# First attention of a two-layer network in half steps, with two strips of each score pass side by side

## The chip, the cores and the metric

The kernel runs on one core of one Trainium2 chip. The metric is the device time of one execution in microseconds (us), lower is better; a shown time is the median of the runs of one kernel. The core has a matrix engine (PE, with its weight loads listed apart as PEld), a vector engine (DVE), a scalar engine (ACT), GpSimd (POOL) and a queue engine for transfers (SP). Each engine works through its own list of instructions in the order of the program; semaphores hold an instruction until what it needs is there. Products of PE land in PSUM, which the kernel uses as eight banks of 128 x 512 float32 numbers; DVE and ACT read them from there.

## What is computed

Eight sequences of 512 positions with 256 channels go through two layers, each an attention and a feed-forward part with modulated layer norms and gates. The change touches the first attention alone: 16 query heads of 16 channels, one key and one value head shared by all of them, rotary positions, a causal mask.

```python
h = _layernorm(x, axis=-1) * (1 + ca) + sa
q = (h @ Wq + bq).reshape(B, T, 16, 16); k = (h @ Wk + bk)[:, :, None, :]; v = (h @ Wv + bv)[:, :, None, :]
q, k = _apply_rope(q, sin, cos, 16), _apply_rope(k, sin, cos, 16)
att = jnp.einsum('bthd,bThd->bhtT', q, k) / math.sqrt(16)
att = jax.nn.softmax(jnp.where(causal, -jnp.inf, att), axis=-1)
out = jnp.einsum('bhtT,bThd->bthd', att, v).reshape(B, T, 256)
x = x + ga * (out @ Wo + bo)
```

After it come a layer of 16 experts that each choose 64 positions of every sequence, a linear attention with running sums, and three rounds of a coupling network.

## The kernel before, in words

**Two passes over the scores.** For each sequence, called a batch here, the score products are made twice. The first pass (`maxima`, lines 637 to 691) makes the scores with queries on the partitions and takes each row's maximum. The second pass (`heads_of`, lines 693 to 760) makes them again with keys on the partitions, subtracts the maxima by small bf16 products, takes the exponential, and multiplies with the values. The heads lie in four groups of 32 partitions: strip j (0 to 3) holds the scores made from partitions 32j to 32j+31. A product with 32 rows uses one of four row sets of PE, so products of different strips can run beside each other. A strip is one PSUM bank of 512 columns.

**Rounds.** The causal blocks of 512, 384, 128 and 256 columns are packed into five rounds of one or two blocks that fill 512 columns; there are two halves g of the heads, so ten rounds in each pass. A round of the first pass: four strips get their score products (line 644), then four or eight bf16 products with all 128 rows, an identity times a triangular mask of -1e30 (line 652), hide the upper triangle of the diagonal blocks, and four DVE reductions (lines 659, 666) read the strips. A round of the second pass: four strips of score products (line 723), the small products that subtract the maxima (line 731), four exponentials on ACT into `e` (line 738), one or two selections on POOL that zero the masked corner (line 742). Four value products with 128 rows by 32 columns (line 708, `values`) collect a batch's output; three of them stand between rounds, the fourth at the end.

**Steps.** The order on every engine is written out by hand: a batch is a Python generator, `Steps.run` takes one piece of each live generator per step, in order of rank, and the instructions stand in that order on each engine. A new batch starts every 15 steps (`steps.start_every(15, batch, 1)`). Batch b goes through `made_ready` (layer norm, transposes at line 263, QKV products at 564, rotation on DVE and POOL, transposes at 604 and 614), `maxima`, `heads_of`, and `finished` (transposes at 774 and 789, normalisation on DVE at 779 and 781, output product at 803, second layer norm, router product at 829). So in one step there stand a piece of `finished` of batch b-1 or so, a piece of `made_ready`, one round of the second pass of batch b, and one round of the first pass of batch b+1. The experts start when the second pass of the last batch is done (`until("heads", B - 1)`).

**Banks.** All PSUM tiles of this part come from one pool of eight banks (`net.mm()`). A new tile takes the bank that was released first, and its first product waits for the instruction that read the former tile last. A step takes four strips for each pass and one or more tiles for the other pieces, so nine or ten in all. Work for the end of the maxima (lines 673 to 689) turns them into three bf16 parts, transposes these (686) and copies them (`mT`, 689), which the second pass of that batch needs.

Of the kernel before, what the change touches and what calls it, by code (L numbers as in the profile page):

```python
# [11 lines left out]
F32 = mybir.dt.float32  # L12
# [8 lines left out]
P = 128  # L21
# [345 lines left out]
class Steps:  # L367


    def __init__(self):  # L370
        self.starters, self.lanes, self.past = [], [], set()
        self.count = 0

    def start(self, lane, rank):

        self.lanes.append([rank, self.count, lane])
        self.count += 1

    def start_every(self, every, batch, rank):
        def starter():  # L380
            for b in range(B):
                self.start(batch(b), rank)
                for _ in range(every):
                    yield

        self.starters.append(starter())

    def rank(self, rank):

        self.now[0] = rank  # L390
# [5 lines left out]
    def run(self):  # L396
        while self.starters or self.lanes:
            self.starters = [s for s in self.starters if next(s, self) is not self]
            for at in sorted(self.lanes, key=lambda at: at[:2]):
                self.now = at  # L400
                if next(at[2], self) is self:
                    self.lanes.remove(at)

# [11 lines left out]
def layer0(net, steps):  # L415
# [48 lines left out]
    for j in range(4):  # L464
# [8 lines left out]
    mask = wp.tile([P, P], F32, name="mask_qk")  # L473
    nc.gpsimd.memset(mask, 0.0)
    nc.gpsimd.affine_select(
        out=mask, in_=mask, compare_op=ALU.is_ge, fill=NEG,
        base=0, pattern=[[-1, P]], channel_multiplier=1,
    )
    maskb = wp.tile([P, P], BF16, name="maskb")
    nc.vector.tensor_copy(maskb, mask)  # L480
# [148 lines left out]

    def maxima(b, kT, qT):  # L630
# [6 lines left out]
        for g in range(2):  # L637
            for blocks in rounds:
                strips = [net.mm() for _ in range(4)]
                for n, (p, a, at) in enumerate(blocks):  # L640
                    i = tile_of[a]
                    nk = (i + 1) * P
                    for j in range(4):
                        nc.tensor.matmul(  # L644
                            strips[j][:, at : at + nk],
                            qT[rows_of(j), g, i * P : (i + 1) * P], kT[rows_of(j), p, :nk],
                            start=(n == 0), stop=False, skip_group_check=True,
                        )
                for j in range(4):
                    for p, a, at in blocks:  # L650
                        last = at + tile_of[a] * P
                        nc.tensor.matmul(  # L652
                            strips[j][:, last : last + P], net.identb, maskb,
                            start=False, stop=True, skip_group_check=True,
                        )
                p, a, _ = blocks[0]
                for j in range(4):
# [35 lines left out]
    def heads_of(b, kT, qT, mT):  # L693
# [7 lines left out]
        def values(n):  # L701

            av = net.mm()
            for a in range(4):
                c = chunk_of[a]
                e, at = parts.pop((n, a))
                for j in range(4):
# [4 lines left out]
                    )  # L712
            o = op.tile([P, T], F32, name=f"oT{n}")
            nc.scalar.copy(o, av)
            oT.append(o)

        for g in range(2):
            for r, blocks in enumerate(rounds):
                strips = [net.mm() for _ in range(4)]
                for n, (p, a, at) in enumerate(blocks):  # L720
                    c = chunk_of[a]
                    for j in range(4):
                        nc.tensor.matmul(  # L723
                            strips[j][:, at : at + T - c * P],
                            kT[rows_of(j), p, c * P : (c + 1) * P], qT[rows_of(j), g, c * P :],
# [1113 lines left out]
```

## Time and profile before

| | |
|---|---|
| median of 3 runs | 1199.55 us (1198.77 to 1199.65) |
| profiled execution | 1200.28 us, of which the span of the core is 1198.3 us |
| mean granted TensorE clock | 0.965 |
| busy: PE, DVE, ACT, POOL | 1105.7, 710.3, 554.7, 496.8 us |
| first product of the first pass, batches 0 to 7 | 28.4, 72.7, 124.7, 183.3, 241.8, 300.3, 358.8, 417.4 us |
| first product of the second pass, batches 0 to 7 | 70.4, 122.8, 181.4, 239.9, 298.4, 356.9, 415.6, 469.1 us |
| last value product of batch 7 | 504 us |
| experts, then second layer's attention and coupling | about 504 to 730, then to 1198 us |

The first attention thus takes the first 504 us or so of the span. A *period*, from the first product of the first pass of one batch to that of the next, is 58.5 us for batches 2 to 6. A busy time in a table of groups counts overlapping records of one group once; a matmul's record lasts longer than the time after which the next one may start, so the sum over groups is a little more than the time they take. The weight loads (PEld) run beside the products.

### The profile page before, as it was taken

What the parts mean: (1) busy time and instruction counts of PE and PEld (TensorE: products, weight loads), DVE (VectorE), ACT (ScalarE), POOL (GpSimd) and SP (SyncE); (2) the same over time, 40 slices, a digit from 0 to 9 for tenths busy, and PEclk for the clock granted to TensorE, in tenths of its full rate; (3) what the DMA queues carried; (4) which work ended last, traced back from release to release, by engine and by line L of the source; (5) the groups of instructions that cost most, each with busy time, mean ns of one, the idle gap of its engine ahead of it and who ended that gap; (6) DMA issues with size and microseconds to landing.
All of it is one profiled execution on the core that took longest, in us unless ns stands there. A gap on an engine that the chain in (4) does not pass through costs nothing. (4 is left out here: it accounts for less than half of the span.)

```text
span 1198.3 us, 22165 instructions
## 1 busy us (share of the span) xinstructions
PE 1105.7 (92%) x8942; PEld 712.4 (59%) x8942; DVE 710.3 (59%) x1463; ACT 554.7 (46%) x1024; POOL 496.8 (41%) x539
## 2 busy tenths in 40 slices
PE   4879999999999999879898999799999988999996
PEld 3545666665666665468776876466666665444433
DVE  4967676666666766723562223666667655556765
ACT  2145656565555547614332244444444324555444
POOL 3023334434343425466787787355556444000000
PEclk8889999999999999989999999899999998999998
DMA  6200000100001010198757944400000000000202
GB/s 215 65 9 2 2 28 25 28 24 28 27 26 42 12 48 23 52 295 234 180 83 187 245 79 60 107 7 6 5 6 5 6 2 1 0 1 1 71 0 71
DMA packets 67974, 69.09 MB, mean 58 GB/s; under 512 B 10216, under 2 KB 64544, under 8 KB 67872
## 3 DMA queue, kind: packets, MB, share of 16 engines
q1 hardware_dynamic: 55024, 49.32, 13.2%
q0 software_dynamic: 12288, 16.79, 8.2%
q8 instruction: 70, 1.15, 0.4%
q10 hardware_dynamic: 560, 1.58, 0.4%
q14 instruction: 32, 0.26, 0.1%
HBM read 46.38 MB, written 21.01 MB: 56 GB/s over the span
## 5 line engine op out<-in xcount | busy, mean ns | idle before, releaser
L738 ACT ACTIVATE e<-mm 128x512 f32<-128x512 f32 x320 | 164.7, 605 | 103.2 <-PE mm L731 99.3
L666 DVE TENSOR_REDUCE pm<-mm 128x4 f32<-128x512 f32 x256 | 158.8, 683 | 84.9 <-PE mm L652 84.6
L742 POOL TENSOR_SCALAR_AFFINE_SELECT e<-e 128x512 f32<-128x512 f32 x128 | 80.3, 645 | 252.3 <-ACT e L738 252.3
L644 PE MATMUL mm<-kT,qT 32*128 32x128 f32 (+3 forms) x1024 | 136.5, 467 | 1.5 <-DVE o_tok L781 1.4
L1112 POOL DMA_INDIRECT xs<-y,slot x64 | 101.4, 1585 | 38.9 <-issue 14.6
L723 PE MATMUL mm<-qT,kT 32*128 32x128 f32 (+3 forms) x1024 | 106.5, 465 | 0.0
L644 PEld LDWEIGHTS mm<-kT,qT 32*128 32x128 f32 x1024 | 75.2, 187 | 44.8 <-DVE pm L666 10.9
L1625 PE MATMUL mm<-g,cn_w 128*128 128x512 f32 x192 | 98.5, 627 | 0.0
L708 PE MATMUL mm<-e,vaug 128*32 128x512 f32 (+3 forms) x1024 | 77.3, 436 | 3.9 <-POOL e L742 2.5
L723 PEld LDWEIGHTS mm<-qT,kT 32*128 32x128 f32 x1024 | 57.1, 184 | 26.8 <-issue 10.6
L1044 POOL DMA_INDIRECT tok<-xg,gidx x64 | 63.4, 991 | 19.3 <-issue 17.5
L1668 DVE SCALAR_TENSOR_TENSOR m<-th,slope,g 128x512 f32<-128x512 f32 x48 | 34.0, 748 | 60.5 <-ACT th L1661 60.5
L1445 POOL TENSOR_SCALAR_AFFINE_SELECT am<-am 128x1024 f32<-128x1024 f32 x32 | 44.3, 1386 | 56.0 <-ACT am L1443 56.0
L1089 PE MATMUL mm<-ew,hid 128*128 128x256 f32 x256 | 63.9, 394 | 3.5 <-ACT hid L1078 3.5
L1076 DVE TENSOR_SCALAR hid<-mm,eb 128x512 f32<-128x512 f32 x32 | 24.0, 751 | 70.8 <-PE mm L1069 41.0
L1078 ACT ACTIVATE hid<-mm,eb 128x512 f32<-128x512 f32 x32 | 22.0, 686 | 92.5 <-PE mm L1069 77.2
L1069 PE MATMUL mm<-tokT,ew 128*128 128x256 f32 x256 | 62.0, 386 | 0.0
L1069 PE MATMUL mm<-hid,ew 128*128 128x256 f32 x256 | 61.4, 383 | 0.0
L1273 PE MATMUL mm<-hT,w1qkv 128*128 128x512 f32 x128 | 60.5, 618 | 0.0
L1094 DVE SCALAR_TENSOR_TENSOR y<-mm,eb,gb 128x512 f32<-128x512 f32 x32 | 23.9, 746 | 59.7 <-PE mm L1089 49.8
L1625 PEld LDWEIGHTS mm<-g,cn_w 128*128 128x128 f32 x192 | 33.6, 195 | 41.3 <-issue 39.5
L1089 PEld LDWEIGHTS mm<-ew,hid 128*128 128x128 f32 x256 | 48.4, 199 | 10.3 <-ACT hid L1078 4.3
(245 smaller groups left out, 2195.3 us busy)
## 6 DMA issues: line engine op xcount, KB each, us to landing
ew<-in_L_ffn_w SPq DMA_DIRECT2D x72, 256.0 KB
x<-in_L_attn_x SPq DMA_DIRECT2D x8, 512.0 KB
xs<-x SPq DMA_DIRECT2D x8, 512.0 KB
xg<-xh SPq DMA_DIRECT2D x8, 512.0 KB
x<-xs SPq DMA_DIRECT2D x8, 512.0 KB
out<-res SPq DMA_DIRECT2D x16, 256.0 KB
ga_row<-gate_a SPq DMA_DIRECT2D x16, 128.0 KB
mod_row<-rows SPq DMA_DIRECT2D x16, 128.0 KB
```

Source lines behind the costliest of these rows:

```text
L644: nc.tensor.matmul(strips[j][:, at : at + nk], qT[rows_of(j), g, i * P : (i + 1) * P], kT[rows_of(j), p, :nk], start=(n == 0), stop=False, ...
L666: nc.vector.tensor_reduce(pm[:, j, 2 * g + p, first : first + 4], strips[j].rearrange("q (a k) -> q a k", k=P), AX.X, ALU.max,)
L708: nc.tensor.matmul(av[32 * j : 32 * j + 32, c * P :], va[:, c, :], e[:, j, at : at + T - c * P], start=(a == 0), stop=(a == 3), skip_group ...
L723: nc.tensor.matmul(strips[j][:, at : at + T - c * P], kT[rows_of(j), p, c * P : (c + 1) * P], qT[rows_of(j), g, c * P :], start=(n == 0), ...
L738: nc.scalar.activation(e[:, j, :], strips[j], AF.Exp, scale=scale)
L742: nc.gpsimd.affine_select(out=own, in_=own, compare_op=ALU.is_ge, fill=0.0, base=0, pattern=[[0, 4], [1, P]], channel_multiplier=-1,)
L1044: nc.gpsimd.indirect_dma_start(out=tok[i][:, n, :], out_offset=None, in_=net.xg[half], in_offset=bass.IndirectOffsetOnAxis(ap=self.gidx[ha ...
L1069: nc.tensor.matmul(ps[:, o * C : (o + 1) * C], w[i][n][:, k, o * P : (o + 1) * P], src[:, k, :], start=(k == 0), stop=(k == 1),)
L1089: nc.tensor.matmul(ps[:, n * C : (n + 1) * C], hid2[i][:, k, n * P : (n + 1) * P], w[i][2][:, k, :], start=(k == 0), stop=(k == 1),)
L1112: nc.gpsimd.indirect_dma_start(out=net.xs[2 * half + n], in_=y[i][:, n, :], in_offset=None, out_offset=bass.IndirectOffsetOnAxis(ap=self.s ...
L1273: nc.tensor.matmul(ps, w[:, k, n * P : (n + 1) * P], hT[:, k, :], start=(k == 0), stop=(k == 1))
L1625: nc.tensor.matmul(ps, w1[:, k, o * P : (o + 1) * P], g[k][bb], start=(k == 0), stop=(k == 1),)
```

## The change

What it does, in words:

- `Steps.run` now counts half steps. A generator has a period (`every`) and a phase: most take a turn in every second half step, `made_ready` in the odd ones, `finished` in the even ones, the two score passes in all. A batch starts every 30 half steps, the second layer's attention every 34.
- A score pass may hand over groups of products instead of issuing them. `run` collects those of the two passes and issues them in turns: a group of the second pass, a group of the first, and so on. Then the readers are issued.
- A round is done in two half steps of two strips: strips 0 and 1 of the first pass beside 2 and 3 of the second, then the other way round. Both passes follow one ORDER of ten rounds with three pauses; in a pause the second pass makes a value product (in two halves), the first pass does nothing.
- The mask is four products of 32 rows for each strip, on the strip's own row set, in place of one or two of 128 rows. Their operands (`picks`, `hides`, 128 x 320 in bf16) are shifted views. Two diagonal blocks of a strip are one product of 256 columns. There are 160 mask products in a batch, with 64 before.

```diff
@@ Steps
-    def start_every(self, every, batch, rank):
+    def start_every(self, every, batch, rank, phase=0):
...
     def run(self):
+        step = 0
         while self.starters or self.lanes:
             self.starters = [s for s in self.starters if next(s, self) is not self]
+            together = []
             for at in sorted(self.lanes, key=lambda at: at[:2]):
+                if step % at[3] != at[4] % at[3]:
+                    continue
+                self.now = at
+                got = next(at[2], self)
+                if got is self:
+                    self.lanes.remove(at)
+                elif got is not None:
+                    together.append((at, got))
+            for groups in itertools.zip_longest(*(got for _, got in together), fillvalue=()):
+                for issue in itertools.chain(*groups):
+                    issue()
+            for at, _ in together:
                 self.now = at
                 if next(at[2], self) is self:
                     self.lanes.remove(at)
+            step += 1
@@ layer0
-    mask = wp.tile([P, P], F32, name="mask_qk")
...
-    maskb = wp.tile([P, P], BF16, name="maskb")
-    nc.vector.tensor_copy(maskb, mask)
+    wide = P + 2 * 96
+    picks = wp.tile([P, wide], BF16, name="picks")
+    hides = wp.tile([P, wide], BF16, name="hides")
+    for t, fill, keep in ((picks, 1.0, ALU.not_equal), (hides, NEG, ALU.is_ge)):
+        f = wp.tile([P, wide], F32, name="picks_f")
+        nc.gpsimd.memset(f, 0.0)
+        nc.gpsimd.affine_select(
+            out=f, in_=f, compare_op=keep, fill=fill,
+            base=96, pattern=[[-1, wide]], channel_multiplier=1,
+        )
+        nc.vector.tensor_copy(t, f)
+
+    def shifted(t, j, part):
+        at = 96 + 32 * (j - part)
+        return t[32 * j : 32 * j + 32, at : at + P]
@@ maxima
+    ORDER = (0, 1, 2, 3, None, 4, 5, None, 6, 7, 8, None, 9)
...
-                for j in range(4):
-                    for p, a, at in blocks:
-                        last = at + tile_of[a] * P
-                        nc.tensor.matmul(
-                            strips[j][:, last : last + P], net.identb, maskb,
-                            start=False, stop=True, skip_group_check=True,
-                        )
...
+            def hide(j, part):
+                nc.tensor.matmul(
+                    strips[j].rearrange("q (n k) -> q n k", k=P)[:, own],
+                    shifted(picks, j, part),
+                    shifted(hides, j, part).unsqueeze(1).to_broadcast([32, len(ends), P]),
+                    start=False, stop=(part == 3), skip_group_check=True,
+                )
+
+            groups = [
+                [functools.partial(score, j, n, *block) for j in js]
+                for n, block in enumerate(blocks)
+            ]
+            groups += [[functools.partial(hide, j, part) for j in js] for part in range(4)]
+            return strips, groups
+
+        for q in ORDER:
+            if q is None:
+                yield
+                yield
+                continue
+            g, blocks = q // 5, rounds[q % 5]
+            p, a, _ = blocks[0]
+            for js in ((0, 1), (2, 3)):
+                strips, groups = scores(g, blocks, js)
+                yield groups
+                for j in js:
...
@@ heads_of
+            groups = [
+                [functools.partial(score, j, n, *block) for j in js]
+                for n, block in enumerate(blocks)
+            ]
+            groups += [[functools.partial(less, j, *block) for j in js] for block in blocks]
+            return strips, groups
+
+        for q in ORDER:
+            if q is None:
+                yield from values(len(oT))
+                continue
+            g, r = divmod(q, 5)
+            blocks = rounds[r]
+            e = ep.tile([P, 4, T], F32, name=f"e{r % 3}", bufs=1 if r == 2 else 2)
+            for js in ((2, 3), (0, 1)):
+                strips, groups = scores(g, blocks, js)
+                yield groups
+                for j in js:
+                    nc.scalar.activation(e[:, j, :], strips[j], AF.Exp, scale=scale)
+                if js[0] == 0:
+                    for p, a, at in blocks:
+                        own = e[:, :, at : at + P]
+                        nc.gpsimd.affine_select(
...
@@ batch
-        steps.rank(1)
+        steps.rank(1, 2, 1)
         kT, qT = yield from made_ready(b)
-        steps.rank(3)
+        steps.rank(3, 1)
         mT = yield from maxima(b, kT, qT)
         past.add(("maxima", b))
-        steps.rank(2)
+        steps.rank(2, 1)
         oT, wg = yield from heads_of(b, kT, qT, mT)
...
-    steps.start_every(15, batch, 1)
+    steps.start_every(30, batch, 1, 1)
...
-    steps.start_every(17, batch, 2)
+    steps.start_every(34, batch, 2)
```

`score` and `less` are the products of lines 644, 723 and 731 before, for one strip. `values` yields once in its middle and once at its end.

## The prediction

> **What bounds the kernel now.** I read the page's busy table first (PE leads), then the windows cut at the first products of the first pass, one period each, since the change touches only the first 504 us.
>
> ```profile
> PE 1105.7 (92%) x8942; PEld 712.4 (59%) x8942; DVE 710.3 (59%) x1463; ACT 554.7 (46%) x1024; POOL 496.8 (41%) x539
> 72.70:124.70 52.00, 50.68 (x564) 30.33 (x556) 35.73 (x68) 29.43 (x56) 18.08 (x24) 1.00 0.01 2
> 241.80:300.30 58.50, 58.09 (x617) 36.29 (x616) 39.88 (x84) 33.59 (x65) 23.91 (x30) 1.00 0.09 27
> 417.40:469.10 51.70, 50.69 (x568) 30.13 (x568) 32.44 (x67) 27.61 (x54) 16.17 (x23) 1.00 0.09 30
> 469.10:504.00 34.90, 32.53 (x367) 18.39 (x370) 26.98 (x71) 26.67 (x53) 17.07 (x24) 1.00 0.21 59
> ```
>
> After the length come PE, PEld, DVE, ACT and POOL. In a full period (58.5 us) PE's records cover 58.09, but a record also runs on while products wait for banks. The groups of that period show which:
>
> ```profile
> L644 PE MATMUL mm<-kT,qT 32*128 32x384 f32 (+3 forms) x128 | 17.0, 459 | 0.3 <-DVE o_tok L781 0.3
> L723 PE MATMUL mm<-qT,kT 32*128 32x512 f32 (+3 forms) x128 | 12.9, 461 | 0.0
> L708 PE MATMUL mm<-e,vaug 128*32 128x512 f32 (+3 forms) x128 | 9.7, 436 | 0.1
> L652 PE MATMUL mm<-maskb,identb 128*128 128x128 bf16 x64 | 5.3, 221 | 0.0
> L731 PE MATMUL mm<-mT,minus 32*128 32x384 bf16 (+3 forms) x64 | 5.2, 294 | 0.0
> ```
>
> L644 and L723 do equal products, yet the first pass takes 17.0 and the second 12.9. The ten PE lines of this table that aren't scores, subtraction or masks sum to 27.7 (L708 9.7, L564 4.3, L803 3.9, L774 2.8, L263 2.6, L789 1.5, L614 1.3, L829 0.6, L604 0.6, L686 0.4). Ten score steps thus get 58.5 - 27.7 = 30.8. The timeline of one step:
>
> ```profile
> 222.17 1.15 PE L723 MATMUL mm<-qT,kT 32*128 32x256 f32 x16
> 223.13 0.40 PE L731 MATMUL mm<-mT,minus 32*128 32x256 bf16 x8
> 223.35 2.04 PE L644 MATMUL mm<-kT,qT 32*128 32x512 f32 x8
> 225.32 0.40 PE L652 MATMUL mm<-maskb,identb 128*128 128x128 bf16 x4
> 225.65 1.22 PE L723 MATMUL mm<-qT,kT 32*128 32x512 f32 x8
> ...
> 212.83 1.15 PE L644 MATMUL mm<-kT,qT 32*128 32x384 f32 x16
> 213.91 0.62 PE L652 MATMUL mm<-maskb,identb 128*128 128x128 bf16 x8
> 214.37 1.92 PE L564 MATMUL mm<-wqkv,hT 128*128 128x288 f32 x7
> ```
>
> Starts, not records, tell the cost. Four strips of scores take 0.96 (222.17 to 223.13), subtraction 0.22 (to 223.35), so a second-pass round is 1.18. A first-pass round that waits for nothing takes 1.08 to its masks (212.83 to 213.91); at 223.35 it took 1.97. Four masks take 0.33 (225.32 to 225.65), eight 0.46 (213.91 to 214.37), or 0.058 each. Of ten rounds four have four masks, six have eight: 0.41 on average. Unobstructed: 10 x (1.18 + 1.08 + 0.41) = 26.7. So **4.1 us of a period are waits for banks**, which the weight loads of periods 124.7 to 417.4 put down to DVE:
>
> ```profile
> PEld mm L644 <- DVE pm L666: 6.0, 20, 0.3
> PEld mm L644 <- DVE qkv L568: 3.2, 10, 0.4
> PEld mm L723 <- DVE pm L666: 2.7, 10, 0.4
> ```
>
> **The change, part by part. PE's own work.** A half step holds two strips of each pass on four row sets, as long as one round of one pass: 1.08 with the way back to 128-row work. Behind it stand four mask products in series on their row set: 0.23 for a one-block round (0.058 each; the two subtractions beside them need 0.22), 0.46 for a two-block round, since its product has 256 columns (an estimate: twice the 128-column one). So a half costs 1.31 (8 of 20) or 1.54 (12 of 20). Eight halves are followed by the next half with no other PE work between; there the way back (0.12) and a weight load (about 0.1) fall away: 0.2 each. Sum: 8 x 1.31 + 12 x 1.54 - 8 x 0.2 = 27.4, against 26.7. The masks leave the 128-row array but not PE's time: product for product the change gains nothing; all depends on the waits.
>
> A weight load could stand ahead of each mask product on the same rows. In the trace the eight loads of line 731 run from 222.92 to 223.25, under score products of the same rows (222.17 to 223.32), so I take them as hidden; the other end is rival B.
>
> The Trainium skill speaks against that: "TensorE: Matmul & The Clock Gate", Part 3, says a weight load overlaps running products only where the row group differs. By that rule each half would grow by four loads and the sum would end where rival B's does; by the row just named it grows by nothing and the sum stays, and the row decides.
>
> **Waits left.** The built order shows what stands where in the 30 half steps.
> - Rounds 0 to 3 (8 halves): DVE has 16 reductions at 0.62 (four at 225.59 take 2.48), four pairs L779 and L781 (0.248 + 0.425), four L531 and L532 (0.406 + 0.182): 9.9 + 2.7 + 2.4 = 15.0. PE has 4 x 1.31 + 4 x 1.54 - 0.6 = 10.8 of scores and L774 2.8, L789 1.1, L686 0.4: 15.1. With both full, a bank is sometimes late; between 0 and 2 I take 0.8. In a half the two passes go in turns, so a late bank of the first pass also holds the second blocks and subtractions of the second, and ACT behind them.
> - Rounds 6 to 8 (6 halves, no other PE work): PE 4 x 1.54 + 2 x 1.31 - 1.0 = 7.8; DVE 12 x 0.62 + two L531 and L532 (1.2) + L584 1.44 + L592 0.68 = 10.7. DVE is the bound: 2.9 of wait.
> - Rounds 4, 5 and 9: PE has more to do than DVE (L803, L263, L564), no wait.
>
> Full period: 27.4 + 0.8 + 2.9 = 31.1 against 30.8: **+0.3, five times: +1.5.**
> - The first overlapped period (72.7 to 124.7) lacks `finished`: 52.0 less other PE lines (18.6) is 33.4. After: rounds 0 to 3 by DVE, 9.9 + 2.4 - 0.4 = 11.9, then 5.7, 10.7, 3.1: 31.4. **-2.0.**
> - The last (417.4 to 469.1) lacks `made_ready`: 51.7 - 19.5 = 32.2. After: 10.8 + 0.5, 5.7, 8.6 (no L584, L592), 3.1: 28.7. **-3.5.**
>
> **Ends, where one pass is alone.** In 469.1 to 504 only the second pass runs: ten rounds of 1.18, now twenty halves with two row sets idle. Eight halves have 128-row work on both sides (9.4); six pairs follow directly on opposite row sets and may share (1.3 each, 7.8): 17.2 - 11.8 = **+5.4**. If they don't share, 23.6, +11.8; ACT (26.67 of 34.9) covers none of it for sure. At the start the first round's second half falls behind the wait for the second modulation, and PE is cold there:
>
> ```profile
> 34.99 0.27 PE L150 MATMUL mm<-ident,s 8*128 8x8 f32 x1 [3.95 <-DVE s L145]
> ```
>
> Two reductions (1.28) move behind 35, and scores of two strips take as long as four took (2.05 at 35.23, granted clock 0.50); after that DVE (35.94 of 44.7) is the bound as before: **+2.0** (0 to 4). The larger mask tables cost POOL and DVE under 2 us before 7.1, where POOL waits 2.48 for DVE: nothing. After 504 the engines' orders differ only in how the last `finished` stands beside the first experts; SP passes the same transfers. Nothing.
>
> **Sum.** 1.5 - 2.0 - 3.5 + 5.4 + 2.0 = +3.4 on the profiled 1200.3; the median of the runs lies 0.7 lower: 1203.0. Within 0.2% (2.4 us) is what a measurement can't tell from no change.
>
> **Rivals.**
> - A, faster: the waits go. For: DVE idles 18.6 and ACT 24.9 in a period, and the two now read at the same time. Against: rounds 6 to 8 above. Then each full period loses 30.8 - 27.4 = 3.4, the first 6.0, the last 4.8: -27.8, plus the ends 7.4: about 1179.
> - B, much slower: mask products don't hide their weight loads (L652's last 0.099): 0.4 per half in the 14 halves that DVE doesn't bound, 5.6 per period, seven periods: +39, about 1242. It decides once a mask product of 128 columns follows the one before on its row set by over 0.1. Against: the loads of line 731.
> - C: the passes don't run beside each other, every half doubles its 0.96: +19 a period, about 1337. Against: row sets run past each other in the trace (L731 starts at 305.01 while L723 of other strips still starts at 305.08 and 305.22).
>
> **Chances.** Forecast 0.46 (own range 1196 to 1211), A 0.32, B 0.14, C 0.03, unforeseen 0.05. Faster: 0.08 of the forecast, 0.31 of A, 0.01 of the rest, 0.40. Same: 0.12 and 0.02 of A and the rest, 0.14. Slower: 0.46. The range takes most of A and the lower half of B: 1178 to 1222.
>
> **What would show it.** A full period of 58 to 59.5 us; first period near 50, last near 48; DVE without gaps in rounds 6 to 8; mask products 0.06 or 0.12 apart on a row set; the second pass of the last batch taking 40 us, not 35. If the period falls below 56, A holds; above 61, B. A granted clock under 1.00 in the periods would also make the sum wrong.

## The result, and the profile after

The changed kernel takes 1259.8 us (1254.1 to 1265.4) beside 1199.6 for the kernel before: 1.050 times as long, 95% interval 1.045 to 1.0555. The profiled execution took 1257.1 us, its span is 1254.9, the mean granted clock 0.939. The page of the changed kernel, its busy table and its row of the granted clock in 40 slices of 31.4 us:

```profile
PE 1131.5 (90%) x9710; PEld 737.5 (59%) x9710; DVE 750.3 (60%) x1464; ACT 562.3 (45%) x1024; POOL 503.5 (40%) x541
...
PEclk9689998989898989898989899889999998899998
```

DVE is busy 40 us longer than before, with one more instruction. The four runs lie 11 us apart, and the slower a run, the lower its mean granted clock (0.941 in the fastest, 0.931 in the slowest). The windows, cut at the first products of the first pass as before (length, PE, PEld, DVE, ACT, POOL, granted clock, transfers):

```profile
80.80:132.30 51.50, 48.78 (x653) 31.95 (x652) 37.33 (x67) 30.39 (x56) 18.39 (x24) 0.96 0.01 2
263.10:328.30 65.20, 59.28 (x717) 38.50 (x716) 46.39 (x84) 34.52 (x64) 24.47 (x30) 0.94 0.08 24
458.60:515.90 57.30, 50.63 (x679) 33.17 (x678) 40.07 (x69) 29.19 (x54) 18.97 (x23) 0.95 0.09 24
515.90:557.40 41.50, 40.45 (x367) 21.21 (x370) 26.41 (x71) 27.12 (x53) 12.28 (x22) 0.93 0.13 42
```

A full period is 65.2 us, not 58.5. PE's records leave 5.9 us of it empty (0.4 before), DVE's work has grown from 39.9 to 46.4 with the same 84 instructions, and the clock is no longer 1.00. The timeline of the changed kernel ahead of that period's first product shows the first two; the columns are start, duration, engine and line:

```profile
254.63 1.86 DVE L731 CAST m<-mx 128x64 bf16<-128x64 f32 x1
256.53 2.25 DVE L734 TENSOR_TENSOR rest<-mx,m 128x64 f32<-128x64 f32 x1
258.82 2.27 DVE L731 CAST m<-rest 128x64 bf16<-128x64 f32 x1
261.12 0.23 DVE L734 TENSOR_TENSOR rest<-rest,m 128x64 f32<-128x64 f32 x1
261.38 0.24 DVE L731 CAST m<-rest 128x64 bf16<-128x64 f32 x1
...
253.88 2.52 POOL L911 TENSOR_TENSOR xh<-xh,mod_row 128x1024 f32<-128x1024 f32 x1
256.37 2.33 POOL L826 TENSOR_TENSOR x<-x,bo_g 128x1024 f32<-128x1024 f32 x1
258.66 2.33 POOL L911 TENSOR_TENSOR xh<-xh,mod_row 128x1024 f32<-128x1024 f32 x1
...
255.14 0.62 PE L898 MATMUL mm<-hT,wg_r 128*32 128x128 f32 x16
261.68 0.61 PE L740 MATMUL mm<-identb,m 128*128 128x128 bf16 x4 [5.92 <-DVE m L731]
```

Five tiny DVE operations make the three bf16 parts of the maxima. The last two take 0.23 us each; the first three take 1.86 to 2.27, and each ends as one of three long GpSimd operations ends (256.4, 258.7, 261.0). PE has finished everything else at 255.8 and waits 5.92 us for the last cast. Then the clock falls (windows of 3 us, same columns):

```profile
255.00:258.00 3.00, 0.76 (x24) 0.40 (x16) 2.97 (x2) 1.02 (x3) 3.00 (x2) 1.00 0.03 8
258.00:261.00 3.00, 0.00 (x0) 0.00 (x0) 2.97 (x2) 0.00 (x0) 2.99 (x2) 0.69 0.16 40
261.00:264.00 3.00, 2.32 (x12) 1.58 (x16) 2.20 (x9) 0.59 (x1) 0.00 (x0) 0.50 0.60 189
264.00:267.00 3.00, 3.00 (x30) 1.58 (x26) 1.28 (x3) 1.09 (x2) 0.00 (x0) 0.67 0.00 0
```

The clock record is 0.50 from 259.1 to 266.0, 6.8 us, and the same length recurs in every full period; before the change it was 1.00 from 72.6 to 509.5. In the kernel before, that chain of five operations stood at 233.05 to 236.6, during the second pass's last round, and the long GpSimd operations began at 237.08, so it missed them (its lines are shown further down). The changed passes share one ORDER with pauses; the first pass now ends with the second, and its chain stands at the period's end, where the batches' long GpSimd operations stand as well.

**Where the time went**, profiled executions, us. "Start" is the first score product, "fill" runs to the second batch's first pass, "rest" is counted from the start of the last value product:

| | start | fill | first overlapped | full period | last overlapped | drain | rest | span |
|---|---|---|---|---|---|---|---|---|
| before | 28.4 | 44.3 | 52.0 | 58.5 | 51.7 | 34.9 | 694.4 | 1198.3 |
| changed | 31.8 | 49.0 | 51.5 | 65.2 | 57.3 | 41.5 | 697.5 | 1254.9 |
| e1 | 32.6 | 57.7 | 51.5 | 60.7 | 51.9 | 41.8 | 688.1 | 1227.0 |
| e2 | 31.9 | 55.9 | 51.1 | 60.0 | 51.8 | 41.9 | 696.5 | 1229.0 |
| e3 | 31.7 | 63.3 | 54.6 | 65.2 | 56.3 | 38.7 | 695.1 | 1265.5 |
| e6 | 32.0 | 57.5 | 49.4 | 57.7 | 50.1 | 39.9 | 687.3 | 1204.9 |
| e13 | 28.0 | 43.9 | 47.6 | 57.7 | 50.1 | 34.3 | 695.5 | 1188.1 |

Of the 56.6 us the five full periods hold 33.6, the two ends 14.7 (start 3.4, fill 4.7, drain 6.6), the last overlapped period 5.6, the rest 3.1; the first overlapped period is 0.5 shorter.

### The profile page after: what moved, and what is told of

It reads as the page before. It is cut to its first block, busy times and chain, and to the rows that moved or that the text cites. A ratio compares the mean times of both kernels' runs of the same rounds, so it can differ in the third digit from the quotient of the medians.

```text
span 1254.9 us, 23708 instructions
## 1 busy us (share of the span) xinstructions
PE 1131.5 (90%) x9710; PEld 737.5 (59%) x9710; DVE 750.3 (60%) x1464; ACT 562.3 (45%) x1024; POOL 503.5 (40%) x541
## 5 line engine op out<-in xcount | busy, mean ns | idle before, releaser
L812 ACT ACTIVATE e<-mm 128x512 f32<-128x512 f32 x320 | 172.7, 597 | 135.6 <-PE mm L788 80.2
L677 PE MATMUL mm<-kT,qT 32*128 32x384 f32 (+3 forms) x1024 | 216.6, 493 | 0.0
L720 DVE TENSOR_REDUCE pm<-mm 128x4 f32<-128x512 f32 x256 | 163.0, 682 | 84.1 <-PE mm L687 72.2
L780 PE MATMUL mm<-qT,kT 32*128 32x512 f32 (+3 forms) x1024 | 194.2, 475 | 0.0
L817 POOL TENSOR_SCALAR_AFFINE_SELECT e<-e 128x512 f32<-128x512 f32 x128 | 85.6, 689 | 257.2 <-ACT e L812 257.2
L677 PEld LDWEIGHTS mm<-kT,qT 32*128 32x128 f32 x1024 | 106.3, 194 | 20.2 <-ACT e L812 3.5
L780 PEld LDWEIGHTS mm<-qT,kT 32*128 32x128 f32 x1024 | 94.5, 190 | 29.7 <-issue 16.0
L687 PE MATMUL mm<-hides,picks 32*128 32x256 bf16 (+1 forms) x1280 | 105.4, 256 | 0.0
L687 PEld LDWEIGHTS <-picks 32*128 32x128 bf16 x1280 | 75.5, 98 | 36.4 <-issue 31.2
L1737 DVE SCALAR_TENSOR_TENSOR m<-th,slope,g 128x512 f32<-128x512 f32 x48 | 34.0, 747 | 60.5 <-ACT th L1730 60.5
L788 PE MATMUL mm<-mT,minus 32*128 32x128 bf16 (+3 forms) x512 | 67.5, 304 | 0.0
L1147 ACT ACTIVATE hid<-mm,eb 128x512 f32<-128x512 f32 x32 | 22.0, 687 | 90.0 <-PE mm L1138 72.6
```

Source lines behind the costliest of these rows:

```text
L677: nc.tensor.matmul(strips[j][:, at : at + nk], qT[rows_of(j), g, i * P : (i + 1) * P], kT[rows_of(j), p, :nk], start=(n == 0), stop=False, ...
L687: nc.tensor.matmul(strips[j].rearrange("q (n k) -> q n k", k=P)[:, own], shifted(picks, j, part), shifted(hides, j, part).unsqueeze(1).to_ ...
L720: nc.vector.tensor_reduce(pm[:, j, 2 * g + p, first : first + 4], strips[j].rearrange("q (a k) -> q a k", k=P), AX.X, ALU.max,)
L780: nc.tensor.matmul(strips[j][:, at : at + T - c * P], kT[rows_of(j), p, c * P : (c + 1) * P], qT[rows_of(j), g, c * P :], start=(n == 0), ...
L788: nc.tensor.matmul(strips[j][:, at : at + T - c * P], minus[rows_of(j), 2 * g + p, :], mT[rows_of(j), c * P :], start=False, stop=True, sk ...
L812: nc.scalar.activation(e[:, j, :], strips[j], AF.Exp, scale=scale)
```

## The experiments

### What stretches the period

**e1: the long GpSimd operations moved.**

```diff
+            if i == 0:
+                nc.gpsimd.tensor_tensor(
+                    xt, xt, bg.unsqueeze(1).to_broadcast([P, NT, C]), ALU.add
+                )
...
+        for _ in range(3):
+            yield
         for row, how in zip(mod_rows, (ALU.mult, ALU.add)):
...
```

(`x+=bo_g` at the end of the second pass goes, and `xh` gets a third buffer)

> The changed kernel with GpSimd's three long operations at the end of a period moved away: x+=bo_g goes from the end of the second pass into the second step of the batch's last part, the two operations xh*row and xh+row start three of the batch's steps (six half steps) later, with a third buffer for xh. Nothing else is changed. Theory 1 (these three operations hold up VectorE's chain that makes the three parts of m, TensorE runs empty for it, and then gets half its clock): the three casts and two subtractions take 0.22 to 0.24 us each again, no stretch of granted clock 0.50 is left between 75 and 510 us, a full period falls from 65.2 to 57-58 us, and the time from 1257 to about 1207 (1198 to 1218). Theory 2 (the half steps themselves or the mask products are dearer than I reckoned, and the chain is only where the delay shows): the stall moves to another wait, a full period stays over 62 us, the time over 1240. Theory 3 (VectorE's 46 us of work in a period are the bound): period 60 to 62, time 1220 to 1240.

Measured: 1229.4 us, ratio 1.027 (1.025 to 1.030); full period 60.7. That is a good half of what theory 1 expected, and both numbers lie in theory 3's ranges; the timeline of e1 says why, and e6 below decides against theory 3:

```profile
258.24 2.08 DVE L731 CAST m<-mx 128x64 bf16<-128x64 f32 x1
260.35 0.23 DVE L734 TENSOR_TENSOR rest<-mx,m 128x64 f32<-128x64 f32 x1
260.62 0.24 DVE L731 CAST m<-rest 128x64 bf16<-128x64 f32 x1
...
257.87 2.36 POOL L865 TENSOR_TENSOR x<-x,bo_g 128x1024 f32<-128x1024 f32 x1 [0.36 <-DVE bo_g L300]
```

Two of the three operations are away, and two of the three stretched ones are normal again. The third, `x+=bo_g`, stands later in the program, but nothing is ahead of it in GpSimd's queue: it starts as soon as `bo_g` is there, and the first cast ends with it. The wait before the transposes is 2.07 us, with 3.4 us of clock at 0.50 in three of the five full periods. The fill took 8.7 us longer than in the changed kernel (the clock stayed at 0.50 until 70.5 instead of 54.3), which the prediction for e1 had not allowed for. That is not the edit's doing alone: in e11 below, where only two tables get other names, the clock stayed at 0.50 until 67.1 and the fill took 56.9.

**e2: the same operations, each in four.**

```diff
-        nc.gpsimd.tensor_tensor(
-            net.x[b], net.x[b], bg.unsqueeze(1).to_broadcast([P, NT, C]), ALU.add
-        )
+        for i in range(NT):
+            nc.gpsimd.tensor_tensor(net.x[b][:, i], net.x[b][:, i], bg, ALU.add)
```

(and the two operations on `xh2` likewise)

> The changed kernel with the same three long GpSimd operations left where they are, but each cut into four of 128x256. Theory 1a (a VectorE operation of the chain waits for the end of the one GpSimd operation that it meets): each of the casts and subtractions is held for at most one quarter, 0.6 to 0.85 us instead of 2.25, the chain is shorter by some 4 us, the wait before the transposes of m stays under the length after which the clock falls, or falls for less; full period 58 to 61 us, time 1215 to 1235. Theory 1b (the two engines share a rate, and the stretch is in proportion to GpSimd's work): the chain takes as long as before in all, and the time stays at 1250 to 1260. Theory 2 (half steps or masks): no change, 1250 to 1265.

Measured: 1233.7 us, 1.030 (1.028 to 1.0325), full period 60.0. The timeline of e2:

```profile
255.55 0.24 DVE L731 CAST m<-mx 128x64 bf16<-128x64 f32 x1
255.82 0.63 DVE L734 TENSOR_TENSOR rest<-mx,m 128x64 f32<-128x64 f32 x1
256.49 0.66 DVE L731 CAST m<-rest 128x64 bf16<-128x64 f32 x1
...
254.78 2.95 POOL L911 TENSOR_TENSOR xh<-xh,mod_row 128x256 f32<-128x256 f32 x4
```

Four of the chain's operations now take 0.63 to 0.66, a little less than a quarter of a GpSimd operation (0.73). Each waits out the one GpSimd operation that it meets, however long that is, and then goes: in the changed kernel, e1 and e2 every stretched operation of the chain ends 0.08 to 0.10 us after the GpSimd operation that ran when it started. The wait before the transposes is 1.90 us. Theory 1b, a shared rate, falls. The Trainium skill, "SBUF — State Buffer", section "Who interferes with whom", describes this: DVE and GpSimd share a port pair as an exclusive lock for a whole instruction, and a DVE operation with two SBUF inputs or a cast between SBUF tiles can need it. These rows agree, and so do the reductions that read PSUM: about 0.68 us each with or without GpSimd beside them.

**e3: work for PE during the chain.**

```diff
+        ps = net.mm()
+        for _ in range(9):
+            nc.tensor.matmul(
+                ps, qT[:, 0, :P], kT[:, 0, :], start=True, stop=True, skip_group_check=True,
+            )
         left = mx
```

> The changed kernel with nine products of 128x512 float32 added that nothing reads, put ahead of the transposes of m, so that TensorE has some 5.6 us of work while VectorE's chain runs. The chain's three operations stay stretched at about 2.25 us. Theory 1 (half of the loss is the granted clock, and it falls because TensorE runs empty): the granted clock stays 1.00 from 75 to 510 us, a full period falls by the clock's share, from 65.2 to some 62 us, and the time to 1230 to 1242. Theory 4 (the clock falls for another reason, such as the load of the products in turns): the 0.50 stretches stay, the products only add their time, 1257 to 1300.

Measured: 1269.1 us, 1.059 (1.056 to 1.062). Neither theory fits: the time is in the range of theory 4, but the clock was 1.00 from 88 to 576, as theory 1 has it, and the full period stayed at 65.2. The timeline of e3:

```profile
267.40 7.89 PE L730 MATMUL mm<-kT,qT 128*128 128x512 f32 x18
...
270.33 0.24 DVE L736 CAST m<-mx 128x64 bf16<-128x64 f32 x1
...
275.82 2.37 POOL L916 TENSOR_TENSOR xh<-xh,mod_row 128x1024 f32<-128x1024 f32 x1 [6.22 <-PE mm L265]
```

Each product is two records, and the nine took 7.9 us instead of 5.6. They stood ahead of the transposes of `xh` (L265), which release GpSimd's first long operation; that came at 275.82, 4 us after the chain had ended. So this run took away the stretched chain too, and paid 7.9 us of products for it. 65.2 - 7.9 = 57.3 is then a period with neither the stretch nor the fall of the clock. With PE busy through the chain the clock did not fall, so the empty wait is what brings it down.

**e6: e1 with `x+=bo_g` behind a select.**

```diff
-            if i == 0:
+            if i == 2:
```

> As e1_pool_later, but x+=bo_g is put behind two more steps of the batch's last part, so that it stands behind GpSimd's first select of the new period in its queue and can't start at once when bo_g is there, which in e1_pool_later still held the first cast for 2.08 us. Theory 1: all five operations of the chain take 0.22 to 0.24 us, the wait before the transposes of m falls from 2.2 us to about 0.2, no 0.50 stretch of the clock is left in the full periods, a full period falls from 60.8 to 56.5-57.8, the time from 1229 to about 1203 (1195 to 1212), the fill apart, whose clock may come up earlier or later by some 10 us of the record. Theory 3 (VectorE bound): no gain, 1222 to 1232.

Measured: 1208.0 us, 1.009 (1.007 to 1.011). Timeline and window of e6:

```profile
252.27 0.24 DVE L731 CAST m<-mx 128x64 bf16<-128x64 f32 x1
252.55 0.23 DVE L734 TENSOR_TENSOR rest<-mx,m 128x64 f32<-128x64 f32 x1
```

```profile
254.40:312.10 57.70, 57.46 (x713) 38.08 (x712) 40.61 (x84) 34.46 (x65) 24.25 (x30) 1.00 0.09 27
```

The whole chain is at 0.23 to 0.24, the wait is 0.24 in every full period, there is no clock loss from 93 to 591, and the full period is 57.7, 0.8 under the kernel before. Theory 3 falls. So the meeting of chain and GpSimd cost 65.2 - 57.7 = 7.5 us a period: 5.7 of wait and, the remainder, 1.8 from the clock (6.8 us at half, of which 2.5 fell into the wait).

### The parts of the change

**e5: no turns.**

```diff
-            for groups in itertools.zip_longest(*(got for _, got in together), fillvalue=()):
-                for issue in itertools.chain(*groups):
+            for _, got in together:
+                for issue in itertools.chain(*got):
                     issue()
```

> The changed kernel, but the products of the two half steps of one step are not taken in turns: all of the second pass's half step, then all of the first pass's. Theory 1 (the turns work, two strips of each pass run side by side): without them the two half steps run one behind the other, a half of a pass alone took 0.97 to 1.05 us in the fill at full clock, so a step takes about 2.0 instead of 1.3 to 1.5 us, a full period 65 plus some 10 to 13 us, time 1325 to 1360. Theory 2 in the form of rival C (the passes never ran side by side): no change, 1245 to 1265.

Measured: 1324.1 us, 1.106 (1.104 to 1.108); full period 72.5. Theory 2 falls, but the loss is 7 us a period, not 10 to 13, and not all of it need be the turns': the clock is at 0.50 for 10.2 or 13.7 us around each full period here, for 6.8 in the changed kernel. A price of the turns with the clock at 1.00 throughout was not measured.

**e4, e10, e7: the masks.** The masks as before, in the changed kernel and in e6, and the new ones alone in the kernel before:

```diff
-            def hide(j, part):
+            def hide(j, n):
                 nc.tensor.matmul(
-                    strips[j].rearrange("q (n k) -> q n k", k=P)[:, own], shifted(picks, j, part),
-                    shifted(hides, j, part).unsqueeze(1).to_broadcast([32, len(ends), P]),
+                    strips[j][:, ends[n] * P : ends[n] * P + P], net.identb, maskb,
...
```

> The changed kernel with the masks of the first pass as before the change: products over all 128 rows, one for each masked block, behind the scores of a half step, instead of four 32-row products. Theory 1: the masks are not the cause, the period moves by -2 to +2 us and the chain and the clock are as in the changed kernel, time 1245 to 1275. Theory 2 in the form of rival B (the 32-row mask products don't hide their weight loads and cost over 0.1 us each): without them a full period falls by 3 us or more, time 1215 to 1235.

> e6_pool_later2 with the masks as before the change (128-row products). It prices the masks in turns where the wait before the transposes of m is gone. Theory 1: a 128-row product on all four row sets stops both passes' products; e4_old_masks showed 0.1 us at each change between the second pass's subtractions and a mask (26 of them, 2.6 us) and a full period 3.1 us longer: full period 60 to 61.5 instead of 57.7, time 1222 to 1235. If the 3.1 us were only a longer stall: 57.5 to 58.5 and 1205 to 1214.

> The kernel before with only the masks changed: four 32-row products to each strip, in turns over the four strips, instead of one 128-row product for each masked block. The 128-row masks and the changes to and from them take 3.66 + 0.94 = 4.6 us of a full period there. Theory 1 with the masks as a gain by themselves: 4 times 0.06 to 0.107 us on four row sets at once, 0.24 to 0.43 a round, 3.4 a period, so 0.5 to 1.5 us less a period, time 1188 to 1197. Theory 1 with the masks as a gain only in turns (e4_old_masks lost 3 us a period without them): 1197 to 1203. Theory 2 (the masks are dear): 1205 or more.

Measured: e4 1280.5 us, 1.070 (1.067 to 1.074), full period 68.5; e10 1221.7, 1.018 (1.015 to 1.021), 60.5; e7 1204.6, 1.007 (1.005 to 1.010), 59.0. In turns the 32-row masks are worth 60.5 - 57.7 = 2.8 us a period without the stall, and 3.3 with it, so e4 lies outside both of its theories and on the side opposite to rival B's. In the four-strip rounds of the kernel before they cost 0.5 a period, and e7's time lies between its theories; part of that is its later start. The timeline of e10 shows what they avoid:

```profile
263.39 0.28 PE L779 MATMUL mm<-mT,minus 32*128 32x256 bf16 x2
263.60 0.37 PE L670 MATMUL mm<-kT,qT 32*128 32x256 f32 x1
263.91 0.29 PE L680 MATMUL mm<-maskb,identb 128*128 128x128 bf16 x2
264.13 0.28 PE L779 MATMUL mm<-mT,minus 32*128 32x256 bf16 x2
264.34 0.29 PE L680 MATMUL mm<-maskb,identb 128*128 128x128 bf16 x2
264.46 0.61 PE L831 MATMUL mm<-ident,oT 128*128 128x128 f32 x4
```

The 128-row masks (263.91, 264.34) stand on all four row sets, ahead of and behind a pair of 32-row subtractions (264.13). Their starts don't mix with the subtractions': each pair begins 0.21 or 0.22 us after the one before, where in e13 below (72.82 to 72.87) 32-row masks and subtractions start 0.01 us apart.

e7 also moved its start by 2.2 us, with this timeline:

```profile
7.88 0.36 POOL L478 MEMSET picks_f<- 128x320 f32 x1 [3.41 <-DVE even_odd L499]
...
9.49 0.33 POOL L543 TENSOR_SCALAR bn_rstd<-bn_mv 128x4 f32<-128x4 f32 x1
...
7.52 0.31 DVE L483 CAST picks<-picks_f 128x320 bf16<-128x320 f32 x1
```

Both tables are built in one tile named `picks_f`. GpSimd can't start the second before DVE has cast the first, that cast stands behind the first batch's statistics in DVE's queue, and GpSimd's `bn_rstd`, at 7.13 before the change, stands behind the table: 9.49.

### The ends

**e11: a name for each table.**

```diff
-        f = wp.tile([P, wide], F32, name="picks_f")
+        f = wp.tile([P, wide], F32, name=f"picks_f{n}")
```

> The changed kernel with nothing changed but that the two float32 tables that the masks are cast from get a name each. Theory: GpSimd's first reciprocal root (bn_rstd) starts about 2 us earlier, and the first product of the first pass comes at 29.5-30.5 us instead of 31.8; the periods as in the changed kernel, time 1250 to 1263. Rival: it is the order of the modulation and the first batch alone that makes the start late: first product at 31.5-32.

Measured: 1256.8 us, 1.047 (1.043 to 1.051); start 30.8 instead of 31.8, between what the theory and its rival had. That is one of the 3.4 us, not two: `bn_rstd` began at 8.89, 1 us earlier, since half of the first batch's statistics now stand a step later on DVE, behind the casts (7.64 us instead of 5.90).

**e8: all four strips where a pass is alone.**

```diff
-            for js in ((0, 1), (2, 3)):
+            for js in ((0, 1), (2, 3)) if b else ((0, 1, 2, 3),):
...
-            for js in ((2, 3), (0, 1)):
+            for js in ((2, 3), (0, 1)) if b < B - 1 else ((0, 1, 2, 3),):
```

> e6_pool_later2, and where a pass runs alone (the first pass of the first batch, the second pass of the last) it takes all four strips in a step, as before the change. Theory: the fill from the first product of the first pass to that of the second batch falls to 43-46 us (44.3 before the change), with the clock at 1.00 again by some 42 us, the drain to 34-37 (34.9 before, 41.5 changed); time 10 to 18 under e6_pool_later2, 1183 to 1200, so at or under the kernel before (1198).

Measured: 1206.3 us, 1.007 (1.005 to 1.009). The time was expected at 1183 to 1200. The drain is 33.9, 6.0 less than in e6, as expected; the fill is 50.5, 7.0 less, but not 43 to 46. The first batch's second pass began at 71.0, but the second batch's first pass only at 83.4, which I put down to the first batch's needing ten steps fewer while the second still starts 30 behind it. Of these 13 us 3.6 were lost in the first overlapped period (53.1), 1.7 in the start and the full periods, and 6.8 in the rest, which is 694.1 here and 687.3 in e6. Why the rest is shorter in e6 was not followed up.

**e9: two steps for each wide one, the first batch ahead of the modulation, and e11's names.**

```diff
+                if len(js) == 4:
+                    yield
...
-                self.start(batch(b), rank, 2, phase)
+                self.start(batch(b), rank, 2, phase if b else 0)
...
-        steps.rank(1, 2, 1)
+        steps.rank(1, 2, 1 if b else 0)
```

> e8_later2_wide with three more edits: the first pass of the first batch takes two of the batch's steps for each wide step, so that the second batch's products are ready when its second pass begins (in e8 the second batch came 12 us after the first one's second pass); the first batch begins in the even steps, ahead of the modulation, as before the change; the two float32 tables that the masks are cast from get a name each, so that GpSimd need not wait for VectorE's first cast to build the second. Theory: first product of the first pass at 28.4-29.5 us (32.0), fill 44-46, first overlapped period 49-50, full periods 57.7, last overlapped 50, drain 34, after it 694: span 1187 to 1196, time 1188 to 1198, so faster than the kernel before (1197.5) by 0 to 0.8%. If the fill's clock stays at 0.50 as in e6 (to 69 us): 1200 or more.

**e12: e9 with three filler products for the first batch and the second modulation two steps later.**

```diff
-        for _ in range(6):
+        for _ in range(8):
             yield
...
+        if b == 0:
+            ps = net.mm()
+            for _ in range(3):
+                nc.tensor.matmul(
+                    ps, qT[:, 0, :P], kT[:, 0, :], start=True, stop=True, skip_group_check=True,
+                )
```

> e9_combined with two edits for its start: three products of 128x512 float32 that nothing reads stand ahead of the first batch's transposes of m, where TensorE waited 2.24 us in e9 and its clock then stayed at 0.50 from 70.7 to 101.4 us; and the second modulation comes two steps later, so that its small product no longer holds the first score product for 1.75 us. Theory (e9 lost its gain to the clock alone: its first overlapped period took 77.2 us instead of 49.4 at full clock): the clock is 1.00 from about 68 us on, the first overlapped period 49.5-52, the first score product at 29-29.5, full periods 57.7, time 1187 to 1194, under the kernel before (1199) by 0.4 to 1%. Rival (the first overlapped period of e9 was long for another reason, such as the second batch's operands): 1210 or more.

Measured: e9 1217.0 us, 1.013 (1.011 to 1.016), start 31.0; e12 1209.1, 1.010 (1.008 to 1.012). In e9 the fill was 39.6, but the first overlapped period 77.2, its first 30.8 us at half clock. In e12 the clock was 1.00 from 71.1 on, and that period still took 62.3 instead of 49.4. So the clock was not the whole of it, and e12's theory fell. Its timeline:

```profile
74.05 1.13 PE L790 MATMUL mm<-qT,kT 32*128 32x512 f32 x4
75.02 0.39 PE L798 MATMUL mm<-mT,minus 32*128 32x512 bf16 x2
75.03 1.13 PE L679 MATMUL mm<-kT,qT 32*128 32x512 f32 x4
75.99 1.02 PE L790 MATMUL mm<-qT,kT 32*128 32x512 f32 x4
```

The first batch had begun one half step early. Its second pass ran a half step ahead of the second batch's first, so in each half step both held the same two strips, and one half follows the other.

**e13 and e14: one more half step of waiting for the first batch; e14 without the filler.**

```diff
         steps.rank(3, 1)
+        if b == 0:
+            yield
```

> e12_combined_warm with one more step of waiting for the first batch ahead of its first pass. In e9 and e12 the first batch begins one step early, so its second pass and the second batch's first pass are one half step apart: both work on the same two strips in every step instead of on different ones. Theory (the half steps run side by side only where the two passes hold different strips): the first overlapped period falls from 62.3 us (clock 1.00 in e12) to 49.5-51.5, the fill to 44-46, the other periods as they were; time 1209 minus 11 to 14, 1193 to 1199, at or just under the kernel before (1197.0). Rival (that period is long for another reason, such as the second batch's late operands): 60 to 63 and 1205 to 1210.

> e13_combined_paired without the three products ahead of the first transposes of m. If TensorE's idle wait there brings the clock down for the following period: 0.50 for 7 to 15 us after it, the first overlapped period 53 to 60, time 3 to 8 over e13. If the 30 us at half clock of e9 came only from both passes being on the same strips: at most one 3.4 us stretch, the time within 2 of e13.

Measured: e13 1190.2 us, **0.994 (0.9925 to 0.9955)**, e14 1191.9, 0.995 (0.993 to 0.996). Both lie a little under the kernel before, by 0.5 to 0.6%, and their intervals leave out 1. Of the 10.2 us that e13's span is shorter, 4.4 lie in the first overlapped period, 4.0 in the five full ones and 1.6 in the last. The timeline of e13 at the place shown of e12:

```profile
71.86 0.70 PE L679 MATMUL mm<-kT,qT 32*128 32x512 f32 x2
71.87 0.70 PE L790 MATMUL mm<-qT,kT 32*128 32x512 f32 x2
72.39 0.59 PE L679 MATMUL mm<-kT,qT 32*128 32x512 f32 x2
72.40 0.59 PE L790 MATMUL mm<-qT,kT 32*128 32x512 f32 x2
72.82 0.22 PE L689 MATMUL mm<-hides,picks 32*128 32x128 bf16 x2
72.83 0.38 PE L798 MATMUL mm<-mT,minus 32*128 32x512 bf16 x2
```

Products of the two passes start 0.01 us apart, and a half of both takes 1.18 us to the next half (73.04), where one half alone took 0.98 in e12. The first overlapped period is 47.6, less than the 49.5 to 51.5 of the theory. In e14 the wait before the transposes was 3.41 us, the clock was at 0.50 from 70.4 to 77.2 and that period took 49.8: a loss of 2.2 us for 6.8 at half clock, between what the two sides of its expectation had. In e9 the wait was 2.24. So its 30 us came with the strips, not with the wait.

## Why the prediction was wrong

The forecast was 1203.0, the result 1259.8, beyond the range. The sign came out, but not for the reason of the forecast: of the 56.6 us 46.8 come from a term that its sum did not have.

- **The step that failed** is "Rounds 4, 5 and 9: PE has more to do than DVE ..., no wait". It compares two sums of work and leaves out the five operations behind round 9, on which the whole next period depends: DVE makes m, PE transposes it, and nothing else is left for PE. In its place the runs showed 5.9 us of wait and 6.8 of half clock. At its usual length the chain would have fitted: the wait is 0.24 in e6. What made it long is that the long GpSimd operations stand in the same place. Against e6 that is 7.5 a full period, 7.2 in the last overlapped and 2.1 in the first: 46.8 of the 56.6 us.
- The trace of before had the sign of it. Its timeline shows the last cast beside a select:

```profile
233.05 0.24 DVE L677 CAST m<-mx 128x64 bf16<-128x64 f32 x1
...
235.95 0.67 DVE L677 CAST m<-rest 128x64 bf16<-128x64 f32 x1
...
235.75 1.35 POOL L742 TENSOR_SCALAR_AFFINE_SELECT e<-e 128x512 f32<-128x512 f32 x2 [4.37 <-ACT e L738]
237.08 2.36 POOL L757 TENSOR_TENSOR x<-x,bo_g 128x1024 f32<-128x1024 f32 x1
```

  A cast that takes 0.24 elsewhere took 0.67, and so it did in five of the seven chains after the fill. The working counted DVE's durations by their usual size and didn't ask what GpSimd does where the chain now stands.
- **The half steps** came near: "27.4" and waits of "0.8" and "2.9" made 58.8 for a full period; without the meeting it is 57.7. In e6 rounds 0 to 3 with their other work take 15.6 (254.40 to 270.01; predicted 15.9) and rounds 6 to 8 take 10.1 (290.01 to 300.08; predicted 10.7). First overlapped 49.4 (50.0), last 50.1 (48.2). Part of this is luck: DVE was busy 12.4 us in that stretch of rounds 0 to 3, where the working had 15.0, and 7.5 in that of rounds 6 to 8, where it had 10.7. In the latter it had two gaps, 1.05 us for PE's masks and 1.73 for GpSimd's `sind`, where it was to have none, and the last four reductions came after the stretch. So "DVE is the bound" is not shown, and which wait makes up the rest of the 10.1 stays open.
- **The masks**' weight loads, taken "as hidden", were: on one row set the products follow 0.06 us (128 columns) and 0.11 us (256) apart. So the row decided rightly against rival B. What the working missed is that they free the other pass: 2.8 us a period. It had written "product for product the change gains nothing".
- **The ends.** The drain's +5.4 was right (39.9 in e6 is +5.0). The start and fill were mis-sized: "+2.0" became 8.1, and "The larger mask tables cost ... nothing" failed: 2.2 us in e7, whose timeline puts them down to one shared tile; in e11 two names won 1.0 of the 3.4. The fill's part goes with the half clock, which lasted to 54.3 instead of 38.5, and to 69 or 70 in e1 and e6, whose fills are the longer for it.
- **Rivals.** A was nearest for the structure: a period without the meeting fell, though by 0.8, not 3.4. B's mark ("above 61, B") was met for another reason; a mark on the period alone can't tell mechanisms apart, the mask products' distance could. C fell: in turns the products of both passes start 0.01 us apart. e12 shows a period in which they follow one another (62.3 against 47.6). The sentence that a clock under 1.00 would upset the sum held, but it had no term and no chance beside it.
- "After 504 ... Nothing": the rest lies between 687 and 698 in all runs (before 694.4, changed 697.5). What moves it was not followed up. It matters for totals: e6 needs 13.7 us more than the kernel before up to its last value product and 7.1 less after it.

## What to carry to other kernels

When an order is changed, look at the shortest chain on which the next stage hangs, and list what every other engine does in the new place: a 0.23 us operation is as long as the longest thing that it can be queued or locked behind. Cut or move the long one, and put something ahead of it in its queue, since a later place in the program alone doesn't delay it. Work meant to run side by side needs a look at which half each part of it holds in every step, at the ends above all.

## What was not expected of the hardware

- PE stayed at half clock though its records covered all of the time. The window of e9 in which both passes held the same strips:

```profile
70.60:101.40 30.80, 30.80 (x186) 17.06 (x183) 10.03 (x18) 10.62 (x20) 5.32 (x10) 0.50 0.00 1
```

  The products show it too: the four records of two strips take 1.71 us from start to start there (72.38 to 74.09) and 0.98 at full clock in e12 (74.05 to 75.03), and that period is 77.2 - 62.3 = 14.9 us longer than e12's. In e14, with the passes on different strips, the clock was back after 6.8 us; in e12, where the same-strip period began at full clock, it did not fall. The fill is alike: where its one pass runs on two strips, the clock was back between 53.0 and 70.5 us in nine profiles, where it runs on four, between 36.5 and 47.3 in seven. For the first batch e8 differs from e6 in that alone: 47.3 and 69.4. What the clock counts as work, no run shows.
- A wait of about 2 us can be enough for a fall. Before the transposes PE waited 2.07 us in e1 and 1.90 in e2, and 3.4 us at 0.50 began there in three and in two of the five full periods. After 5.9 us (the changed kernel) 6.8 us followed in each of the five, after 0.24 (e6, e12 to e14) never any.
- The Trainium skill, "TensorE: Matmul & The Clock Gate", Part 1, has the clock fall after an idle window of about 3.4 us and return after one busy window of that length. All complete stretches at 0.50 in these records are whole multiples of 3.4 us, which agrees with a window of that length. The falls after 2 us of wait do not agree with a window that must be idle throughout, and the 30.7 us do not agree with the return; there the measurements decide.
